# The front of an attention and feed-forward block on one core: program order, a first batch loaded alone, idle matmuls, an earlier norm, and first copies on three queues

## The chip, the cores and the metric

The kernel runs on one core of a Trainium2 chip. The core has a matrix engine (TensorE, PE in the profile; its weight loads are a row of their own, PEld), a vector engine (DVE), a scalar engine (ACT), a general engine (POOL) and a sync engine (SP), each with its own instruction queue that it works through in order. SP, ACT and POOL can also issue DMA transfers. An engine waits for another, or for a transfer, on a semaphore. The metric is the device time of one execution in microseconds (us), as the median of several runs. Smaller is better.

## What is computed

The reference is a block of attention and a gated feed-forward net over 4 batches of 1024 tokens of width 256, with 16 heads of 16. All of it is in 32-bit floats.

```python
def block(x):
    x = x + layernorm(attention(layernorm(x)))
    return x + layernorm(feed_forward(layernorm(x)))

def attention(x):                      # 16 heads of 16
    q, k, v = split(x @ Wqkv.T)
    scores = q @ k.T / sqrt(16)
    e = exp(clip(scores - max(scores), -50, 50))
    return (e / (sum(e) + 1e-6) @ v) @ Wout.T

def feed_forward(x):                   # w1, w2, h1, h2, w3 hold -1, 0 and 1
    h = silu(x @ w1.T * s1) * (x @ w2.T * s2)
    h = gelu(h @ h1.T * s3)
    h = gelu(h @ h2.T * s4)
    return h @ w3.T * s5
```

## The kernel before

`tile_fast` does the whole work; `tile_general` behind it runs only if checks on the data fail, which they do not here. A batch is cut into 2 halves (h) of 512 tokens, a half into 4 tiles of 128 tokens. The 16 heads are 4 groups (g) of 4.

**The front.** For batch 0, and for each half, a *prologue* makes: the norm's statistics (`gather`, L92 and L93: 4 tiles on DVE; `root`, L100 on DVE and L102, a power, on POOL); the normalised tokens `xn` (`apply`, L110, 4 instructions on DVE); their transposes (`pt`, L295, 8 on PE, copied into `xT` by ACT, L256); and, for the first 8 heads, the projections `p` to k and then q (L314, a pair of matmuls each, which the trace shows as 4 records). Each projection is split into a high part (ACT, L256: `ck0hi`, `cq0hi`) and a low part (DVE, L318: `ck0lo`, `cq0lo`). From these, small DMAs build the *stacks* `sk` and `sq` (L403): 16 partitions of 512 elements each, 16 DMAs for k and 16 for q in each half, dealt in turn to the queues of SP and POOL. `pv` (L305) makes the values of two token tiles at a time, 4 steps in all for a batch, and `slots` (L419, POOL) copies them into `vaug`, from which the weighing matmuls read.

**Order.** The set-up of the kernel, down to the rings, is put in order by a scheduler. The part under `with tc.manual_schedule()` stands as written: both halves' norms first, then for each half `apply`, transposes, projections and copies, then two `pv` steps (half of `v`), the first `slots` copy, the stacks of group 1 (`stack(0, 1)`, 32 DMAs on SP) and the output weights (`load_wo`, 16 DMAs on SP).

**The loads.** SP loads `x` of batch 0 (4 DMAs: for each half one of 128 KB and one of 384 KB), then four scales and `w3s`, then `x` of the batches 1 to 3 (12 DMAs). ACT issues one load of the q and k weights, `slotted` (1024 KB), from which POOL copies the used columns into `wqk_sb` (L188), and then `wv`. The pool that holds `slotted` is closed after this, and the pool `work`, in which `xn` and `xT` lie, opens at the same place of memory: the first `xn` waits for the copies out of `slotted`.

**Attention.** The loop goes over 512 score tiles, three at a time. For each, two matmuls make the scores (`s`, L441), ACT takes the exponential (`e`, L442) and four pairs of matmul records add the weighed values (`acc`, L449). The score tiles share three PSUM buffers (`ps`, tag "big"). One call of `side.take()` after each three tiles lets chains of *side steps* advance: at most one step that uses PE in each call, and after as many calls as the step's `gap`. The side steps hold the rest of batch 0's prologue (values, the projections of heads 8 to 15, then *flags*: checks of the size of the scores, `pn` at L350 with its maximum `norm` on DVE at L351, and `pr` at L366), the prologue of the next batch (`later["chain"]`), and checks of the feed-forward weights. Batch 0's side steps, `pn` and `pr` too, take their PSUM from the same three buffers as the scores. At the end of a unit of 16 tiles, `po` (L468, L470) divides by the sums.

**The feed-forward net** runs after all attention, from about half of the span on; none of its lines is touched.

Of the kernel before, what the change touches and what calls it, by code (L numbers as in the profile page):

```python
# [9 lines left out]
F32 = mybir.dt.float32  # L10
# [8 lines left out]
P = 128  # L19
HEADS = 16  # L20
DH = 16
SLOT = 32
# [8 lines left out]
SAFE = 25.0  # L31
FULL = 32.0
EARLY = 256
SPREAD = 32.0
NQ = 512
WIDE = 1024
# [77 lines left out]
def tile_fast(ctx: ExitStack, tc: tile.TileContext, x, wqk, wv, wo, w1, w1s, w2, w2s, h1, h1s, h2, h2s, w3, w3s, out, bad):  # L114
# [22 lines left out]
        t, n = NH + (TPQ - 1) * h, TPQ * h  # L137
        return (slice(n, n + 1), view[:, h : h + 1, :]), (slice(n + 1, n + TPQ), view[:, t : t + TPQ - 1, :])

    def load_x(b):  # L140
        view = x[b].rearrange("(t p) d -> p t d", p=P)
        for h in range(NH):
            for at, tokens in pieces(h, view):
                nc.sync.dma_start(out=xs[b][:, at, :], in_=tokens)

    load_x(0)
    ident = const.tile([P, P], F32, name="ident")
    make_identity(nc, ident)
    ones = const.tile([P, 1], F32, name="ones")
# [10 lines left out]
    misses = const.tile([P, counts + B * 2], F32, name="misses")  # L160
    nc.vector.memset(misses, 0.0)
    rounded = {n: dram.tile(list(w.shape), F32R, name=f"{n}_r") for n, w in weights.items()}
    scales = {}
    for name, w in (("w1", w1s), ("w2", w2s), ("h1", h1s), ("h2", h2s)):
        scales[name] = const.tile([P, HC], F32, name=f"{name}_scale")
        nc.sync.dma_start(out=scales[name], in_=w)
    w3s_sb = const.tile([P, D], F32, name="w3s_sb")
    nc.sync.dma_start(out=w3s_sb, in_=w3s.partition_broadcast(P))


    keep = ctx.enter_context(tc.tile_pool(name="keep", bufs=1))
# [6 lines left out]
    with ExitStack() as actx, ExitStack() as rctx:  # L178
# [4 lines left out]
        wo_sb = aw.tile([P, DC, D], F32, name="wo_sb")  # L183
        with tc.tile_pool(name="load", bufs=1, side="right") as load:
            slotted = load.tile([P, DC, 2, HEADS, SLOT], F32, name="slotted")
            nc.scalar.dma_start(out=slotted, in_=wqk.rearrange("(c p) (k h s) -> p c k h s", p=P, k=2, s=SLOT))
            for c in range(DC):
                nc.gpsimd.tensor_copy(wqk_sb[:, c], slotted[:, c, :, :, 0:DH])  # L188
        nc.scalar.dma_start(out=wv_sb, in_=wv.rearrange("(c p) d -> p c d", p=P))

        def load_wo(c):
            for h in range(HPT):
                r = SLOT * (HPT * c + h)
                nc.sync.dma_start(out=wo_sb[DH * h : DH * (h + 1), c, :], in_=wo[r : r + DH, :])

        for b in range(1, B):
            load_x(b)


        cq = {(w, m, k): keep.tile([P, S], F32R, name=f"c{'qk'[w]}{m}{k}") for w in range(2) for m in range(DC) for k in ("hi", "lo")}  # L200
# [9 lines left out]

        rp = rctx.enter_context(tc.tile_pool(name="ring", bufs=1))
        ring = [rp.tile([P, 2, 2, NQ], F32, name=f"e{i}") for i in range(RING // 2)]

        on = [aw.tile([P, TPQ, D], F32, name=f"on{h}") for h in range(NH)]

# [11 lines left out]
        def check_weights(n, c):  # L227

            k = blocks.index((n, c))
            st = {}  # L230

            def rows(w):
                return w[c * P : (c + rows_at_once[n]) * P, :].rearrange("(i p) d -> p i d", p=P)

            def load():
                st["w"] = work.tile([P, WIDE], F32, tag="w", name="w", bufs=1)
                nc.gpsimd.dma_start(out=st["w"].rearrange("p (i d) -> p i d", i=rows_at_once[n]), in_=rows(weights[n]))

            def cast():
                st["r"] = work.tile([P, WIDE], F32R, tag="wr", name="wr", bufs=1)  # L240
                nc.gpsimd.tensor_copy(st["r"], st["w"])

            def count(j):
                def run():
                    w, r = (t[:, NQ * j : NQ * (j + 1)] for t in (st["w"], st["r"]))
                    i = k * (WIDE // NQ) + j
                    nc.vector.scalar_tensor_tensor(w, w, 1.0, r.bitcast(F32), ALU.mult, ALU.not_equal, accum_out=misses[:, i : i + 1])
                    if NQ * (j + 1) == WIDE:
                        nc.gpsimd.dma_start(out=rows(rounded[n]).bitcast(F32), in_=st["r"].bitcast(F32).rearrange("p (i d) -> p i d", i=rows_at_once[n]))

                return run

            return [Step(load, 0, False), Step(cast, 3, False)] + [Step(count(j), 1, False) for j in range(WIDE // NQ)]
# [140 lines left out]
        def copies(g, w, c0=0, c1=S):  # L394

            m, i = g // GPT, g % 2

            def copy(u, j, n):
                def run(queue):
                    k = "hi" if (j // 2 == 0 if w == 0 else j % 2 == 0) else "lo"  # L400
                    r = (g % GPT) * HPG * DH + (2 * u + n) * DH
                    o = n * ROWS + j * DH
                    queue.dma_start(out=stacks[w, i, u][o : o + DH, c0:c1].bitcast(F32), in_=cq[w, m, k][r : r + DH, c0:c1].bitcast(F32))  # L403

                return run

            return [copy(u, j, n) for u in range(2) for j in range(PARTS) for n in range(2)]

        def stack(b, g):
            for w in (1, 0):  # L410
                for copy in copies(g, w):
                    copy(nc.sync)
            stacked[g % 2] = b, g

        def slots(b, g, t0=0, t1=NT):


            def run():
                nc.gpsimd.tensor_copy(  # L419
                    vaug[g % 2][:, t0:t1, :, 0:DH], cv[:, t0:t1, HPG * DH * g : HPG * DH * (g + 1)].rearrange("p t (h e) -> p t h e", e=DH)  # L420
                )
                slotted[g % 2] = b, g, t1

            return run
# [148 lines left out]
        def begin(b):  # L573

            if b + 1 < B:
                norm, xt, qk, v, flags = prologue(b + 1, misc, to_vector)

                qk1 = sum(qk[1], [])
                qk1[0].gap = 3
                later["rest"] = v, qk1 + [Step(lambda: side.add(flags), 0, False)]  # L580
                later["chain"] = side.add(sum((norm[h] + xt[h] for h in range(NH)), []) + sum(qk[0], []))

        def unit_end(b, g, h):

# [40 lines left out]
        def halves(pool, name):  # L625
            return [pool.tile([P, HC, NQ], F32R, name=f"{name}_{k}") for k in ("hi", "lo")]
# [178 lines left out]
                chain = side.add(finish(n, ffn["a"]), True)  # L805
            side.flush()

        with tc.manual_schedule():
            norm, xt, qk, v, flags = prologue(0, lambda n: ps.tile([P, 2, NQ], F32, tag="big", name=n)[:, 0, :], to_scalar)
            queues = [nc.sync, nc.gpsimd]  # L810
            for h in range(NH):
                for step in norm[h]:
                    step.run()
            for h in range(NH):
                for step in xt[h]:
                    step.run()
                for w, step in zip((1, 0), qk[0][h]):
                    step.run()
                    for i, copy in enumerate(copies(0, w, h * NQ, (h + 1) * NQ)):
                        copy(queues[i % len(queues)])  # L820
            stacked[0] = 0, 0
            for step in v[: len(v) // 2]:
                step.run()
            slots(0, 0, 0, NT // 2)()
            stack(0, 1)
            for c in range(DC):
                load_wo(c)
            side.add(v[len(v) // 2 :] + [Step(slots(0, 0), 0, False), Step(slots(0, 1), 0, False)] + sum(qk[1], []) + [Step(lambda: side.add(flags), 0, False)])
            begin(0)
            side.add([s for k in blocks for s in check_weights(*k)])  # L830
            made = seen = weighed = 0

            def make(end):

                nonlocal made
                for k in range(made, min(end, len(tiles))):
                    assert k - weighed < RING
                    exponentials(k)
                    made = k + 1

            while weighed < len(tiles):
                n = made
                make(n + TURN - side.borrowed)
                if made == len(tiles):
                    n = made
                for k in range(seen, n - 1, 2):
                    rise(k)
                    seen += 2
                while weighed + 2 <= n:
                    b, g, h, c, _ = tiles[weighed]  # L850
                    if c == 0:
                        accs[b, g, h] = ps_acc.tile([P, NQ], F32, tag="acc", name="acc")
                    weigh(weighed, accs[b, g, h])
                    weighed += 2
                    if c == NT - 1:
                        unit_end(b, g, h)
                        if n < len(tiles):
                            break
                make(n + TURN)
                if weighed < len(tiles):  # L860
                    side.take()

            load_weights("h1", range(HC // 2, HC))
            rctx.close()
            ffn["a"] = halves(ctx.enter_context(tc.tile_pool(name="fa", bufs=1, reuse_waits="tile")), "ha")
            feed_forward()


@with_exitstack
# [233 lines left out]
```

## Time and profile before

The median of 3 runs is 1353.05 us (1352.49 to 1354.52). The profiled execution took 1352.66 us, of which its span on the core is 1350.9 us.

| | busy us | share of the span |
|---|---|---|
| PE | 1273.3 | 94% |
| PEld | 799.0 | 59% |
| DVE | 732.5 | 54% |
| ACT | 684.1 | 51% |
| POOL | 159.7 | 12% |

| in the front | us from the span's start |
|---|---|
| first statistics of `x` | 3.45 |
| first `xn` | 11.86 |
| first transpose | 12.33 |
| first projection | 14.53 |
| first copy into a stack (SP) | 18.97 |
| first score matmul | 31.16 |
| first weighing matmul (`acc`) | 35.94 |

A line of the timeline has the start, the length, the engine, the line of the code, the operation, output and inputs, the shapes, and the number of merged instructions; in brackets stands the idle time before them and what ended it. A "q" after an engine's name (SPq) marks its queue issuing DMAs. In a table of windows each pair is the busy time of one engine and, in brackets, its instructions; PEclk is the share of the full clock that TensorE was granted. Ends of matmuls are modelled, so records that follow each other closely can overlap on paper.

### The profile page before, as it was taken

Reading aid. Unit: us, or ns where it says so; the run is one execution under the profiler, and the core shown is the slowest. Engines: PE = TensorE matmul, PEld = TensorE weight load, DVE = VectorE, ACT = ScalarE, POOL = GpSimd, SP = SyncE. Lnnn points to the kernel's source line nnn. Section 1 sums busy time; section 2 is a strip of 40 time slices with the busy share of each in tenths; the row PEclk is TensorE's granted clock in tenths of the full one; section 3 lists DMA queues with packets and bytes.
Section 4 is the critical chain, followed back from the end, with each engine's and each line's share of the span. In section 5 each row is a group of like instructions: output and inputs, shape, how many; then the busy total and the mean of one; then the engine's idle time right before and its main releaser. Section 6 shows DMA issues by size and latency. Waiting matters only on the chain.

```text
span 1350.9 us, 18751 instructions
## 1 busy us (share of the span) xinstructions
PE 1273.3 (94%) x7034; PEld 799.0 (59%) x7034; DVE 732.5 (54%) x1553; ACT 684.1 (51%) x820; POOL 159.7 (12%) x200
## 2 busy tenths in 40 slices
PE   5989999899899999989999999999999999999995
PEld 3333434343343433333478888888888888888884
DVE  3466568755697565735573452725436364363533
ACT  2677787676777678888842231413224141231410
POOL 6241133210421012000000000000000000000000
PEclk9989999899999999999999999999999999999998
DMA  7554344542445432336130000000000000000000
GB/s 215 130 113 110 80 111 91 141 103 60 129 108 133 94 51 48 50 65 195 54 134 1 1 16 0 17 1 0 16 1 16 0 14 3 0 16 0 17 0 19
DMA packets 38390, 79.62 MB, mean 59 GB/s; under 512 B 11280, under 2 KB 21136, under 8 KB 38288
## 3 DMA queue, kind: packets, MB, share of 16 engines
q1 hardware_dynamic: 30384, 52.88, 18.1%
q0 software_dynamic: 7360, 24.12, 5.3%
q10 hardware_dynamic: 544, 1.31, 0.3%
q8 instruction: 58, 0.95, 0.3%
q14 instruction: 44, 0.36, 0.1%
HBM read 28.98 MB, written 15.73 MB: 33 GB/s over the span
## 4 chain that ended last, share of the span: by engine, by line
PE 76%; DVE 12%; ACT 7%; issue 2%; POOL 1%; DMA 1%; SPq 1%; ACTq 0%; POOLq 0%; DVEq 0%
PE ph L686 35%; PE acc L449 13%; PE s L441 8%; ACT e L442 5%; PE p L314 5%; PE pz L739 4%; PE pg L686 3%; PE py L506 2%; PE pv L305 2%; DVE top L458 2%; DVE sg L702 2%; PE po L470 1%; DVE st L92 1%; DVE ha_lo L691 1%; DVE o L259 1%
## 5 line engine op out<-in xcount | busy, mean ns | idle before, releaser
L442 ACT ACTIVATE e<-s 128x1024 f32<-128x1024 f32 x512 | 484.9, 1032 | 143.4 <-PE s L441 128.0
L449 PE MATMUL acc<-e,vaug 128*32 128x512 f32 x2048 | 258.0, 607 | 0.1
L722 ACT ACTIVATE a<-ph,h_scale 128x512 f32<-128x512 f32 x128 | 81.0, 685 | 307.3 <-PE ph L686 307.3
L441 PE MATMUL s<-sq,sk 64*128 64x512 f32 x1024 | 195.9, 452 | 28.0 <-ACT e L442 20.3
L686 PE MATMUL ph<-hb_lo,h 128*128 128x512 f32 x512 | 199.7, 390 | 0.0
L686 PE MATMUL ph<-hb_hi,h 128*128 128x512 f32 x512 | 199.6, 390 | 0.0
L441 PEld LDWEIGHTS s<-sq,sk 64*128 64x128 f32 x1024 | 87.5, 185 | 164.5 <-ACT e L442 121.0
L458 DVE TENSOR_TENSOR top<-top,e 128x512 f32<-128x512 f32 x192 | 146.4, 762 | 29.7 <-ACT e L442 23.4
L102 POOL TENSOR_TENSOR rstd<-ve,minus_half 128x4 f32<-128x4 f32 (+1 forms) x33 | 37.1, 1125 | 772.5 <-DVE ve L100 772.5
L723 DVE CAST ha_hi<-a 128x512 fp32r<-128x512 f32 x64 | 27.1, 424 | 158.2 <-ACT a L722 158.2
L449 PEld LDWEIGHTS acc<-e,vaug 128*32 128x32 f32 x2048 | 49.7, 109 | 106.1 <-issue 96.7
L686 PEld LDWEIGHTS ph<-hb_hi,h 128*128 128x128 f32 x512 | 96.2, 188 | 20.1
L686 PEld LDWEIGHTS ph<-hb_lo,h 128*128 128x128 f32 x512 | 96.2, 188 | 20.0
L686 PE MATMUL ph<-ha_hi,sq 128*128 128x512 f32 x256 | 102.0, 399 | 0.4
L686 PE MATMUL ph<-ha_lo,sq 128*128 128x512 f32 x256 | 100.0, 391 | 0.0
L686 PE MATMUL ph<-ha_lo,sk 128*128 128x512 f32 x256 | 99.9, 390 | 0.0
L686 PE MATMUL ph<-ha_hi,sk 128*128 128x512 f32 x256 | 99.9, 390 | 0.0
L702 DVE SCALAR_TENSOR_TENSOR sg<-pg,w_scale,sg 128x512 f32<-128x512 f32 x64 | 47.1, 746 | 47.9 <-ACT sg L700 47.8
L700 ACT ACTIVATE sg<-pg,w_scale 128x512 f32<-128x512 f32 x64 | 43.3, 688 | 56.7 <-DVE ha_lo L691 47.4
L723 DVE CAST hb_hi<-a 128x512 fp32r<-128x512 f32 x64 | 27.0, 422 | 82.2 <-ACT a L722 82.2
L314 PE MATMUL p<-xT,wqk_sb 128*128 128x512 f32 x128 | 65.1, 635 | 0.2 <-ACT xT L256 0.2
L686 PEld LDWEIGHTS ph<-ha_hi,sq 128*128 128x128 f32 x256 | 48.2, 188 | 12.7 <-DVE sg L702 3.3
(144 smaller groups left out, 1679.6 us busy)
## 6 DMA issues: line engine op xcount, KB each, us to landing
w<-in_h_dram POOLq DMA_DIRECT2D x16, 512.0 KB, 4.4
h_r<-wr POOLq DMA_DIRECT2D x16, 512.0 KB, 3.6
sk<-ck1hi SPq DMA_DIRECT2D x64, 64.0 KB, 2.3
sk<-ck1lo SPq DMA_DIRECT2D x64, 64.0 KB, 2.3
sq<-cq1hi SPq DMA_DIRECT2D x64, 64.0 KB, 2.3
sq<-cq1lo SPq DMA_DIRECT2D x64, 64.0 KB, 2.3
h<-h_r SPq DMA_DIRECT2D x8, 512.0 KB, 7.1
sk<-ck0hi SPq DMA_DIRECT2D x56, 64.0 KB, 2.3
```

The costliest lines, as they stand in the source:

```text
L102: nc.gpsimd.tensor_tensor(rstd[:, :n], ve[:, :n], self.minus_half[:, :n], ALU.pow)
L314: nc.tensor.matmul(pp, wqk_sb[:, c, w, HPT * m : HPT * (m + 1), :], st["xT"][:, c, h * NQ : (h + 1) * NQ], start=c == 0, stop=c == DC - 1)
L441: nc.tensor.matmul(s[:, a, :], stacks[1, g % 2, u][r, c * P : (c + 1) * P], stacks[0, g % 2, u][r, h * NQ : (h + 1) * NQ], start=True, sto ...
L442: nc.scalar.activation(pair(k)[:, u], s, AF.Exp)
L449: nc.tensor.matmul(acc[SLOT * i : SLOT * (i + 1), :], vaug[g % 2][:, c, i, :], pair(k)[:, i // 2, i % 2, :], start=c == 0, stop=c == NT - 1)
L458: nc.vector.tensor_max(top, top if c > 1 else pair(k - 2)[:, :, :, 0:P], pair(k)[:, :, :, 0:P])
L686: nc.tensor.matmul(p, homes[n][c][:, m * P : (m + 1) * P], half[:, c, :], start=c == 0 and k == 0, stop=c == len(homes[n]) - 1 and k == 1)
L700: nc.scalar.activation(sg, p[:, 0, :], AF.Silu, scale=scales["w1"][:, m : m + 1])
L702: nc.vector.scalar_tensor_tensor(sg, p[:, 1, :], scales["w2"][:, m : m + 1], sg, ALU.mult, ALU.mult)
L722: nc.scalar.activation(a, p[:, j, :], AF.Gelu, scale=scales[n][:, m : m + 1])
L723: nc.vector.tensor_copy(o[0][:, m, :], a)
L739: nc.tensor.matmul(p[t], half[:, c, t * P : (t + 1) * P], homes["w3"][c], start=c == 0 and k == 0, stop=c == HC - 1 and k == 1)
```

## The change

All of `tile_fast` after the pools now stands in the order in which it is written (`manual_schedule` opens before the first load). The parts:

1. **Loads.** Only batch 0 is loaded ahead, all on SP: half 0 of `x`, the k half of `slotted` (512 KB), half 1 of `x`, the q half of `slotted`. ACT copies each half into `wqk_sb`. Batch 1's `x` is loaded behind the first copies, and `load_wo`, the batches 2 and 3, the scales and `w3s` behind `stack(0, 1)`.
2. **Idle matmuls.** A memset fills 128x512 of the ring's first buffer with zeros, and four matmuls on it stand first on PE, into the PSUM buffer of the side steps; nothing reads their result.
3. **Early norm.** Half 0's norm and its `xn` now stand ahead of half 1's norm on DVE; half 1's `xn` stands between half 0's k and q copies.
4. **Three queues.** The 16 copies of a k or q half are dealt in groups of eight as ACT, POOL, SP, POOL, SP, POOL, SP, POOL.
5. **Values.** One `pv` step instead of two stands ahead of the first scores; the second, and the first `slots` copy, become the first side steps. The chain of batch 1 starts four calls later.

```diff
-    load_x(0)
+    ctx.enter_context(tc.manual_schedule())
+    load_x(0, [0])
...
-            nc.scalar.dma_start(out=slotted, in_=wqk.rearrange("(c p) (k h s) -> p c k h s", p=P, k=2, s=SLOT))
-            for c in range(DC):
-                nc.gpsimd.tensor_copy(wqk_sb[:, c], slotted[:, c, :, :, 0:DH])
+            for w in (1, 0):
+                nc.sync.dma_start(out=slotted[:, :, w], in_=wqk.rearrange("(c p) (k h s) -> p c k h s", p=P, k=2, s=SLOT)[:, :, w])
+                nc.scalar.copy(wqk_sb[:, :, w], slotted[:, :, w, :, 0:DH])
+                if w:
+                    load_x(0, [1])
...
-        for b in range(1, B):
-            load_x(b)
+        def load_rest():
+
+            for c in range(DC):
+                load_wo(c)
+            for b in range(2, B):
+                load_x(b)
+            for name, w in (("w1", w1s), ("w2", w2s), ("h1", h1s), ("h2", h2s)):
+                nc.sync.dma_start(out=scales[name], in_=w)
+            nc.sync.dma_start(out=w3s_sb, in_=w3s.partition_broadcast(P))
...
+        zeros = ring[0][:, 0, 0]
+        nc.vector.memset(zeros, 0.0)
...
-                later["chain"] = side.add(sum((norm[h] + xt[h] for h in range(NH)), []) + sum(qk[0], []))
+
+                later["chain"] = side.add([Step(lambda: None, 0 if b else 4, False)] + sum((norm[h] + xt[h] for h in range(NH)), []) + sum(qk[0], []))
...
-            queues = [nc.sync, nc.gpsimd]
-            for h in range(NH):
-                for step in norm[h]:
-                    step.run()
-            for h in range(NH):
-                for step in xt[h]:
-                    step.run()
-                for w, step in zip((1, 0), qk[0][h]):
-                    step.run()
-                    for i, copy in enumerate(copies(0, w, h * NQ, (h + 1) * NQ)):
-                        copy(queues[i % len(queues)])
-            stacked[0] = 0, 0
-            for step in v[: len(v) // 2]:
+        queues = [nc.scalar] + [nc.gpsimd, nc.sync] * 3 + [nc.gpsimd]
+
+        idle = misc("idle")
+        for _ in range(WARM):
+            nc.tensor.matmul(idle, zeros[:, 0:P], zeros, start=True, stop=True)
+        normalise = [steps[: TPQ // 2] for steps in xt]
+        for step in norm[0] + normalise[0] + norm[1]:
+            step.run()
+        for h in range(NH):
+            for step in xt[h][TPQ // 2 :]:
                 step.run()
-            slots(0, 0, 0, NT // 2)()
-            stack(0, 1)
-            for c in range(DC):
-                load_wo(c)
-            side.add(v[len(v) // 2 :] + [Step(slots(0, 0), 0, False), Step(slots(0, 1), 0, False)] + sum(qk[1], []) + [Step(lambda: side.add(flags), 0, False)])
+            for w, step in zip((1, 0), qk[0][h]):
+                step.run()
+                for i, copy in enumerate(copies(0, w, h * NQ, (h + 1) * NQ)):
+                    copy(queues[i % len(queues)])
+                if w and h + 1 < NH:
+                    for step in normalise[h + 1]:
+                        step.run()
+        stacked[0] = 0, 0
+        v[0].run()
+        load_x(1)
+        stack(0, 1)
+        load_rest()
+        early = [v[1], Step(slots(0, 0, 0, NT // 2), 0, False)]
+        side.add(early + v[2:] + [Step(slots(0, 0), 0, False), Step(slots(0, 1), 0, False)] + sum(qk[1], []) + [Step(lambda: side.add(flags), 0, False)])
```

The loop over the tiles is moved out by one level of indentation and is otherwise as it was.

## The prediction

> **What bounds the kernel now.** I read the page's slices and chain first, then the timeline of the first 45 us, where the change is, then the stretch of batch 0's checks, and last the granted clock in 3.41 us windows.
>
> ```profile
> PE   5989999899899999989999999999999999999995
> PEclk9989999899999999999999999999999999999998
> PE 76%; DVE 12%; ACT 7%; issue 2%; POOL 1%; DMA 1%; SPq 1%; ACTq 0%; POOLq 0%; DVEq 0%
> ```
>
> PE is full from the second slice on (a slice is 33.8 us), and holds 76% of the chain. So work that leaves the front and goes into the attention isn't saved; only PE's idle and slow time can be. The first slice has half of its time idle.
>
> ```profile
> 0.74 1.97 SPq L144 DMA_DIRECT2D x<-in_x_dram  x4
> 2.75 0.49 SPq L166 DMA_DIRECT2D w_scale<-in_w1s_dram  x1
> 6.21 1.16 POOL L188 COPY wqk_sb<-slotted 128x512 f32<-128x512 f32 x2 [4.05 <-DMA slotted<-in_wqk_dram]
> 7.31 0.43 DVE L92 BATCH_NORM_STATS2 st<-x 128x6 f32<-128x256 f32 x1 [3.22 <-DMA x<-in_x_dram]
> 11.86 1.38 DVE L110 TENSOR_SCALAR xn<-x,mv,rstd 128x256 f32<-128x256 f32 x4
> 14.53 5.82 PE L314 MATMUL p<-xT,wqk_sb 128*128 128x512 f32 x8
> 19.24 0.72 POOL L403 DMA_DIRECT2D sk<-ck0hi  x1 [6.49 <-ACT ck0hi L256]
> 24.07 3.70 PE L314 MATMUL p<-xT,wqk_sb 128*128 128x512 f32 x8 [0.25 <-ACT xT L256]
> 31.16 1.26 PE L441 MATMUL s<-sq,sk 64*128 64x512 f32 x6
> 34.97 0.41 POOL L419 COPY vaug<-cv 128x256 f32<-128x256 f32 x1
> 35.94 1.07 PE L449 MATMUL acc<-e,vaug 128*32 128x512 f32 x8
> ```
>
> The chain to see: loads until 7.31, both halves' statistics until 11.55, `xn` at 11.86. The same eight projection records take 5.82 us cold and 3.70 us warm. POOL issues 32 copies from 19.24 to 34.97 without a gap (0.48 us each), copies `vaug` until 35.38, and only then can `acc` start.
>
> ```profile
> 77.28 0.73 PE L441 MATMUL s<-sq,sk 64*128 64x512 f32 x4
> 80.67 0.80 PE L441 MATMUL s<-sq,sk 64*128 64x512 f32 x2 [2.67 <-DVE norm L351]
> 81.40 1.93 PE L449 MATMUL acc<-e,vaug 128*32 128x512 f32 x8
> ```
>
> ```profile
> 18.83:22.24 3.41, 1.67 (x5) 0.52 (x3) 1.92 (x4) 0.71 (x2) 2.99 (x6) 1.00 0.50 125
> 76.85:80.27 3.42, 1.16 (x12) 0.30 (x4) 3.21 (x10) 2.38 (x3) 0.77 (x1) 1.00 0.60 101
> 80.27:83.68 3.41, 3.00 (x12) 0.91 (x13) 1.23 (x3) 1.02 (x1) 3.39 (x5) 0.50 0.76 112
> 83.68:87.09 3.41, 3.41 (x16) 1.72 (x18) 2.10 (x7) 1.06 (x2) 2.99 (x4) 0.50 0.95 322
> 247.52:250.93 3.41, 1.54 (x12) 0.34 (x10) 3.17 (x13) 3.16 (x4) 0.42 (x1) 1.00 0.64 105
> ```
>
> Second column PE busy, third from the end the clock. A window with PE busy 1.16 or 1.54 us is followed by half clock, one with 1.67 is not; the clock returned after a window that was full, not after one with 3.00. A pause is thus paid twice.
>
> **The change, part by part.** "A" is the start of the first `xn`, 11.86 before.
>
> *Loads and early norm.* Half 0's statistics no longer hold A back: half 0's x, 0.52 MB at the head of the queue, is moved by 3.7 (DMA column: 0.45 MB by 3.5, 0.65 by 4.0); with 0.6 for the landing, three more tiles of statistics and `ve` (7.31 to 9.22, so 1.9) and a power on POOL (1.03), `xn` could start near 7.5. But `xn` lies where `slotted` lay, and waits for ACT's copy of the q half, the last of the six loads. These are the same 2.10 MB as before, which the DMA column completes at 8.0; the first scale, behind x on SP's queue, had landed at 9.15 (issued 2.75, 6.4 to landing). So q lands between 8.0 and 9.15; ACT's copy of 512 elements costs 0.60 (the `xT` row) and 0.1 to start. A is 8.7 to 9.9, and I take 9.7, since the tail counts for the last load: **-2.2**. The far bound is one queue alone at its slowest microsecond, 248 GB/s (13 to 14 us): 2.0 + 8.5, tail 1.1, copy 0.7: A = 12.3, or +0.4. POOL's 1.16 us of copies had cover and goes free.
>
> *Idle matmuls.* The memset lies before any x has landed: nothing. Four matmuls are 8 records of 0.85 us cold (spacing within L314's 5.82), 6.8 us from about 1.4. The clock opens with the end of the first full window, 3.4 to 6.8 us after the start, and halves the rest; they end at 6.5 to 8.2, before A, and delay nothing. If they end later than A + 0.5, the excess is paid in full. What they bring: first transpose at A + 0.47 = 10.2, so PE pauses 2 to 3.7 us. By the windows above (1.54 us busy of 3.41 is too little) the clock mostly closes again, and the projections run cold as before. I take **0**; the other end is warm projections: k's high part was done 7.1 after `xn` cold (18.94) and 5.1 warm (26.69 against 21.62), so -2.0. The Trainium skill, "TensorE: Matmul & The Clock Gate", section "What's actually happening", has the clock close only after an idle window of about 3.4 us and lets a shorter pause pass. The row speaks against it: a pause of 2.67 us closed it. By the rule the projections would mostly stay warm and the sum be lower by those 2.0.
>
> *Three queues.* Of the 32 copies of a half SP now issues 12 instead of 16, ACT 4 and POOL 16 as before. ACT's come in twos behind `ck0hi` and `cq0hi`, at about 0.5 us each (its earlier issues took 0.46 and 0.37), while ACT is idle for 1.12 to 2.44 us behind each of the four anyhow, waiting for PE: nothing; without this cover 1 us per pair. So POOL's chain, 7.4 us after A to the first issue, 15.7 for 32 copies, 0.41 for `vaug`, is unchanged: A + 23.5. The scores come earlier (PE's chain: A + 15.7 with one `pv` less; the last copies at A + 17), but `acc` must wait for POOL. Before it came at A + 24.1, 0.56 after `vaug`; now PE is ready first: **-0.5** (0 to -0.5).
>
> *One `pv` moved.* The front had no room to gain from it (above), so it counts where it lands. By the built order every step shifts by one slot, the row of steps regains the old order at score tile 90 (of 512), and a slot that held no PE step is used up. A slot with a step takes 3.9 to 4.1 us, one without is held by three `e` (2.85) plus waits, 2.9: **+1.2**; from 1.0 to 2.4 (1.93 of PE and a 0.41 wait for the buffer).
>
> *Loads moved behind copies.* On SP, 24 copies, 4 of x1, 32 of group 1 at 0.62: from A + 7.8 to about 55, landed by 57. Group 1 is first read at score tile 32, about 71 now: 14 us spare. Then 29 issues (wo, x2, x3, scales, w3s), 18 us, to 73, when group 2's copies become due; these need not land before tile 64, at about 107, and take 20. Batch 1's statistics stand behind `cq1lo` on DVE, at about 48; x1 lands by 41. All **0**; without cover each us late costs one.
>
> *The check `pn`.* Before, it cost a pause of 2.67 and then half clock: s, acc, po, po, s, acc after it took 0.80, 1.93, 1.12, 1.09, 1.22, 2.27 instead of 0.51, 1.07, 0.66, 0.66, 0.73, 1.92: 2.9 more, 5.6 in all. In the built order it moves from before tile 33 to before tile 39, after a `po`. From `po`'s start T on DVE (62.55 as the model): multiply done T + 3.3 (65.83), two statistics 1.1, `ve` 0.2, power 1.04 to 1.41, two `xn` 0.73, `norm` 0.69: T + 7.2 to 7.5. PE reaches tile 41, which needs that buffer, at T + 5.9. Pause 1.3 to 1.6, and half clock less often, say 3 in 10: 1.6 + 0.9 = 2.5. **-3.1** (0 to -5.6: the old cost, or none). `pr` moves to tile 87; its wait was 0.35 and stays.
>
> The sum: -2.2 - 0.5 + 1.2 - 3.1 = **-4.6**, so 1352.66 - 4.6 = 1348.1 for an execution like the profiled one, which lies 0.4 under the median: **1348.5**.
>
> **The rivals.**
> 1. *The front stays warm.* For it: 18.83:22.24, half idle, kept its clock. Against: the pause is longer. -6.6: 1346.5.
> 2. *The pause at `pn` stays in full.* DVE has `xn` before `norm`, and POOL the power. For it: the same engines made it before; against: the ops counted. -1.5: 1351.5, no change to be told (0.2%, or 2.7 us, is what a measurement of this kernel can tell).
> 3. *Slower: a second half-clock stretch.* `pn` keeps its 5.6, and the other moved check (second `pn`, or `pr`) gets a pause like 250's, 1.7, with 2.9 behind it: -1.5 + 4.6 = +3.1: 1356.2. It decides where a pause leaves PE under 1.6 us busy of a window. For it: the second `pn` already had 0.63 of wait. Against: no x statistics stand before it.
> 4. *No gain at A.* The loads on one queue at 248 GB/s (+0.4 instead of -2.2), the rest as in 2: +1.1: 1354.2.
>
> **How the numbers follow.** Forecast 0.50 (0.42 of it faster, its own range 1346 to 1351), rival 1 0.17 (all faster), rival 2 0.15 (0.04 faster, 0.11 same), rival 3 0.11 (0.09 slower, 0.02 same), rival 4 0.07 (0.06 same, 0.01 slower). The forecast's remaining 0.08 is same. Faster 0.63, same 0.27, slower 0.10. The range runs from rival 1 with `pn` free (1346.5 - 2.5, so 1344) to rival 4 at 1354; outside are rival 3 and the tails.
>
> **What would show it.** First `xn` at 9.7, ended by ACT's copy; idle records over by 8.2, then a pause on PE of over 2 us, and projections again at 0.85 each (warm: 0.43); POOL's 32 copies without gap and `acc` waiting for `vaug`, near 33.3; tile 32 some 2 us earlier than before; a pause of about 1.5 before tile 41 at full clock. From tile 90 on all should be shifted alike. Wrong would be: `xn` after 12, `acc` not ended by POOL, or another half-clock stretch.

## Result and profile after

The changed kernel takes 1349.90 us in the median of 7 executions (1348.01 to 1352.52) against 1353.05 (1350.74 to 1354.52): a ratio of 0.9979, 95% interval 0.9968 to 0.9991. Its profiled execution took 1349.57 us, with a span of 1347.8; before it was 1352.66 with a span of 1350.9.

The timeline of the front after the change (start, duration, engine, line, operation; in brackets the idle time of the engine before it and what ended it):

```profile
1.57 5.66 PE L825 MATMUL idle<-e 128*128 128x512 f32 x8 [1.57 <-DVE heads_bf L227]
...
8.88 0.62 ACT L187 COPY wqk_sb<-slotted 128x512 f32<-128x512 f32 x1 [2.19 <-DMA slotted<-in_wqk_dram]
9.59 1.38 DVE L111 TENSOR_SCALAR xn<-x,mv,rstd 128x256 f32<-128x256 f32 x4 [3.01 <-ACT wqk_sb L187]
10.06 1.73 PE L305 MATMUL pt<-ident,xn 128*128 128x128 f32 x8 [2.82 <-DVE xn L111]
12.11 5.40 PE L324 MATMUL p<-xT,wqk_sb 128*128 128x512 f32 x8 [0.31 <-ACT xT L266]
...
20.08 3.70 PE L324 MATMUL p<-xT,wqk_sb 128*128 128x512 f32 x8 [0.91 <-ACT xT L266]
...
25.44 0.51 PE L451 MATMUL s<-sq,sk 64*128 64x512 f32 x2
27.09 0.93 PE L451 MATMUL s<-sq,sk 64*128 64x512 f32 x4 [1.15 <-DMA sq<-cq0hi]
...
31.28 0.96 POOL L413 DMA_DIRECT2D sq<-cq0lo  x2
32.24 0.41 POOL L429 COPY vaug<-cv 128x256 f32<-128x256 f32 x1
32.70 1.84 PE L459 MATMUL acc<-e,vaug 128*32 128x512 f32 x8 [1.57 <-POOL vaug L429]
```

Up to here it went nearly as forecast. The first `xn` starts at 9.59 (11.86 before), released by ACT's copy of the last weights; in the other ten runs with these loads, described below, it starts between 9.66 and 10.41. The idle records end at 7.23, PE then stands for 2.82 us, and the projections take 5.40 us, cold as before (5.82). POOL issues to 32.24, and the first `acc` waits for `vaug`. The first score is 5.7 us earlier (25.44, 31.16 before), the first `acc` 3.2 (32.70, 35.94).

After that the lead runs away. The table has the start of some `e` tiles (ACT's exponentials, 512 in order) against the same tile of before's profile, in us, from the two traces (negative is earlier; e1, e12 and g1 are runs described below); the last column is the stretch from tile 20 to 92, in which the moved step sits, and behind which both kernels have the same order on PE.

| tile | 0 | 20 | 28 | 60 | 92 | 511 | 20 to 92 |
|---|---|---|---|---|---|---|---|
| changed kernel | -5.43 | -2.14 | +0.79 | -1.31 | -0.16 | -0.39 | +1.98 |
| e1 (one POOL instruction more) | -5.32 | -3.63 | -0.69 | -2.99 | -1.82 | -1.36 | +1.81 |
| e12 (moved step undone) | -4.16 | -3.37 | -3.23 | -5.25 | -5.06 | -4.70 | -1.69 |
| g1 (best) | -3.19 | -3.27 | -2.46 | -6.37 | -5.23 | -14.26 | -1.96 |

So of the span's 3.1 us, the attention holds 0.4. Where it went shows in the timeline from the unit's end near 80 us:

```profile
76.80 2.27 DVE L468 TENSOR_TENSOR top<-top,e 128x512 f32<-128x512 f32 x2
79.00 0.41 DVE L93 BATCH_NORM_STATS2 st<-x 128x6 f32<-128x256 f32 x1
...
80.07 1.45 DVE L257 SCALAR_TENSOR_TENSOR w<-w,wr 128x512 f32<-128x512 f32 x1
...
81.45 1.51 DVE L468 TENSOR_TENSOR top<-top,e 128x512 f32<-128x512 f32 x1
82.89 0.68 DVE L269 TENSOR_SCALAR o<-acc 128x512 f32<-128x512 f32 x1
...
77.49 1.04 POOL L338 TENSOR_TENSOR sq<-cq0hi 128x512 bf16<-128x512 f32 x1
78.50 1.48 POOL L338 TENSOR_TENSOR sq<-cq1hi 128x512 bf16<-128x512 f32 x1
79.94 1.03 POOL L338 TENSOR_TENSOR sq<-ck0hi 128x512 bf16<-128x512 f32 x1
80.93 1.48 POOL L338 TENSOR_TENSOR sq<-ck1hi 128x512 bf16<-128x512 f32 x1
...
78.74 1.07 PE L459 MATMUL acc<-e,vaug 128*32 128x512 f32 x8
83.11 0.63 PE L478 MATMUL po<-ident,top 128*128 128x128 f32 x4 [3.31 <-DVE top L468]
```

PE ends `acc` at 79.81 and waits 3.31 us for DVE's `top`: a pause that the kernel before did not have here. DVE is late, and part of that is that two `top` took 2.27, `w` 1.45 and `top` 1.51 (0.69 each elsewhere) while POOL squared; the statistics beside them took their usual 0.41. The Trainium skill, "GPSIMD Engine Reference", section "1. Specifications", leads one to expect this: POOL shares its SBUF interfaces with VectorE, and there is contention with VectorE's instructions that have two SBUF inputs or run in a 2-port mode (`top` and `w` have two inputs, the statistics one).

The windows of the changed kernel (PE busy second, the clock third from the end) show the price:

```profile
9.00:12.38 3.38, 2.01 (x9) 1.22 (x10) 2.71 (x9) 1.42 (x3) 0.00 (x0) 1.00 0.30 78
29.45:32.86 3.41, 1.82 (x13) 0.74 (x15) 0.00 (x0) 3.19 (x5) 3.41 (x8) 1.00 0.54 122
32.86:36.27 3.41, 3.41 (x12) 1.50 (x5) 0.00 (x0) 0.47 (x1) 0.29 (x1) 0.50 0.78 227
80.65:84.06 3.41, 0.95 (x8) 0.84 (x8) 2.92 (x4) 0.68 (x1) 3.41 (x5) 1.00 0.60 105
84.06:87.47 3.41, 3.41 (x18) 1.09 (x20) 2.87 (x11) 1.94 (x2) 0.07 (x1) 0.50 0.96 247
```

Each of the three pauses is followed by half clock (the first from 12.38 to 15.79); the second, behind the wait before `acc`, and the third, behind the wait for `top`, were not forecast.

And where the rest of the 3.1 us came from stands at the very end. SP's last four stores, and the span, in before and in the changed kernel:

```profile
core 0 of [0], span 1350.9 us
1334.98 5.59 SPq L751 DMA_DIRECT2D out_dram<-z  x4
```

```profile
core 0 of [0], span 1347.8 us
1334.20 5.60 SPq L762 DMA_DIRECT2D out_dram<-z  x4
```

The last store's issue ends at 1340.57 and 1339.80, 0.77 apart; but from there to the end of the span it is 10.3 us and 8.0 us. POOL's records between them, in us:

```
                  wait ends   final drain starts   drain   last store to end
before             1341.19         1343.62          6.41        10.3
changed kernel     1340.27         1340.35          6.27         8.0
```

POOL waits for the stores. The next instruction, a drain, starts 2.4 us later in before, with 8 KB fetches on an instruction queue in the gap, and at once in the changed kernel. Before's trace holds 274 POOL instructions, the changed kernel's 273.

### The profile page after: what moved, and what is told of

The parts are those of the page before. It is cut to its first block, busy times and chain, and to the rows that moved or that the text cites. A ratio compares the mean times of both kernels' runs of the same rounds, so it can differ in the third digit from the quotient of the medians.

```text
span 1347.8 us, 18771 instructions
## 1 busy us (share of the span) xinstructions
PE 1279.4 (95%) x7042; PEld 799.8 (59%) x7042; DVE 736.0 (55%) x1554; ACT 685.1 (51%) x822; POOL 159.2 (12%) x198
## 4 chain that ended last, share of the span: by engine, by line
PE 75%; DVE 12%; ACT 7%; issue 2%; POOL 2%; DMA 1%; SPq 1%; ACTq 0%; POOLq 0%; DVEq 0%
PE ph L697 35%; PE acc L459 13%; PE s L451 8%; ACT e L452 5%; PE pz L750 4%; PE p L324 4%; PE pg L697 3%; PE py L516 2%; PE pv L315 2%; DVE sg L713 2%; DVE top L468 2%; PE po L480 1%; DVE ha_lo L702 1%; DVE st L93 1%; DVE o L269 1%
```

## The experiments

**The end: one POOL instruction more, or fewer (e1, e2, f1).** e1 is the changed kernel with one more:

```diff
             vaug.append(t)
+        nc.gpsimd.memset(vaug[1][:, :, :, DH : DH + 1], 1.0)
```

> The changed kernel with one more POOL instruction (a second memset of the ones columns of the second vaug, early, under the loads), so that POOL has as many instructions as in the kernel before. Theory A (the end of the program depends on where POOL's last instructions lie): the time between the last store's issue and the end of the span is back at 10.3 us (8.0 in the changed kernel, 10.3 before), the rest as in the changed kernel, so the span is 1347.8 + 2.3 = 1350.1 and the time 0.8 us below before. Rival B (the end is chance, or belongs to the stores): the end stays within 0.5 us of 8.0 or varies between executions, the time is 3.1 us below before. Rival C (all of the gain is in the work): the last pz starts 3 us earlier than before.

e2 is the kernel before, with one fewer:

```diff
-            nc.gpsimd.memset(t, 0.0)
-            nc.gpsimd.memset(t[:, :, :, DH : DH + 1], 1.0)
+            on = nc.vector if i else nc.gpsimd
+            on.memset(t, 0.0)
+            on.memset(t[:, :, :, DH : DH + 1], 1.0)
```

> The kernel before with one POOL instruction fewer (both memsets of the second vaug are done by DVE, under the loads), as many as in the changed kernel; nothing of the change is in it. Theory A (place of POOL's last instructions): the time between the last store's issue and the end of the span falls from 10.3 to 8.0 us and the time is 2.3 us below before, so this alone gives most of the changed kernel's 3.1. Rival B (chance, or the stores): end at 10.3, time as before within 0.5 us. Score tile 0 starts at 31.7 and tile 511 as before under both.

Measured: e1 1351.89 us, ratio 1.0000 (0.9992 to 1.0009): the whole gain is gone. e2 1348.53, ratio 0.9973 (0.9961 to 0.9985): as much as the changed kernel, with nothing of the change in it (3.6 us below before, where 2.3 was expected; the interval, 2.0 to 5.3, holds that). The last stores of e1, then of e2:

```profile
core 0 of [0], span 1348.9 us
1333.18 5.60 SPq L763 DMA_DIRECT2D out_dram<-z  x4
```

```profile
core 0 of [0], span 1348.9 us
1335.28 5.59 SPq L752 DMA_DIRECT2D out_dram<-z  x4
```

1348.9 - 1338.78 = 10.1 in e1, 1348.9 - 1340.87 = 8.0 in e2. Is it a count, or a border? f1 repeats e1's memset eight times.

> The changed kernel with eight more POOL instructions (eight small memsets of the second vaug's ones, under the loads). With one more, the end took 10.2 us and the gain was gone. Theory A1 (a border in POOL's program: the wait for the stores and the drain behind it lie on the two sides of it, and the part behind it is fetched only when it is reached; with eight more, both lie behind it and are fetched together while POOL waits anyhow): the end is 8.0 us again and the time is some 3 us below before. Rival A2 (every instruction beyond a count makes the end longer): 10.2 us or more, time as before.

f1: 1347.76, ratio 0.9969 (0.9955 to 0.9984), from the last store to the end 7.8 us. In these runs:

```
POOL instructions   272        273              274          281
kernels             e6, g2     changed, e2      before, e1   f1
wait to drain       0.06       0.06             2.4, 2.5     0.06   us
last store to end   8.0        8.0              10.3, 10.2   7.8    us
```

The other runs have 271 to 273 instructions and end 7.9 to 8.3 us behind the last store. So it is a border in POOL's program that falls between the wait and the drain with 274 instructions only. A smaller gap in the records marks the same place: with 273 it stands one instruction later, behind the drain (0.36 us), with 272 two later (0.39), with 271 three later (0.38). That the drain is then fetched late is read from the fetches in the gap; which unit sets the border was not tried.

**The idle matmuls (e3).** `WARM = 0`.

> The changed kernel without the four idle matmuls. Theory A (they bring nothing, since PE pauses 2.8 us before the projections and runs these cold): the eight projection records of the first half take 5.4 to 5.8 us as with them, score tile 0 starts at 26.3 and the time is that of the changed kernel within 0.5 us. It would even be shorter in the front if a window lost less later: the clock opens 3.4 us or more after the first transposes, so the second half's projections may be cold for 1 us more. Rival D (the idle matmuls do part of the work): score tile 0 at 28.3, 2 us later, and since acc waits for POOL's 32 copies and vaug, acc starts as late as vaug, 32.7 to 34.

1348.56, ratio 0.9975 (0.9966 to 0.9984): as with them. Tile 0 starts at 27.0 (26.3 with them) and `acc` at 33.39 waits 1.58 us for POOL all the same. That is 0.7 us later, as is the first `xn` (10.27 against 9.59), which the idle matmuls don't touch; so they bring nothing. In this run PE did not run at half clock after `top`, and the check's pause came back behind it; its timeline:

```profile
82.18 0.63 PE L478 MATMUL po<-ident,top 128*128 128x128 f32 x4 [3.33 <-DVE top L468]
90.74 0.65 PE L451 MATMUL s<-sq,sk 64*128 64x512 f32 x2 [2.83 <-DVE norm L361]
```

So `pn` had kept its pause. In the changed kernel it looked smaller (0.63), for the most part because PE, at half clock, came to it 1.6 us later after the start of `po`.

**The wait for POOL (e6).** The first copy into `vaug` on DVE, which is idle there:

```diff
-        def slots(b, g, t0=0, t1=NT):
+        def slots(b, g, t0=0, t1=NT, on=nc.gpsimd):
...
-                nc.gpsimd.tensor_copy(
+                on.tensor_copy(
...
-        early = [v[1], Step(slots(0, 0, 0, NT // 2), 0, False)]
+        early = [v[1], Step(slots(0, 0, 0, NT // 2, nc.vector), 0, False)]
```

> The changed kernel with the first copy into vaug on DVE in place of POOL, where it stood behind 32 copies. Theory A (the first acc waits 1.57 us for POOL alone, and the half clock after it, 32.86 to 36.27, is the price of that wait, some 1.7 us): the wait is gone, no half clock around 33, score tile 8 starts 2.5 to 3.3 us earlier than in the changed kernel (36.6 against 39.6); what of that is left at the end of the attention is open, since the lead before it was lost there too. Rival E (the copies on SP end no earlier, or the stacks' landing holds the scores): tile 8 at most 0.5 us earlier. For the whole time A says -1 to -3 us against the changed kernel, E 0.

Tile 8 starts at 35.91 (39.68 in the changed kernel, 38.18 in e1), the wait is gone, and so is the half clock there. The lead of 6.0 at tile 20 fell to 1.0 at tile 92 by the same pauses at `top` (3.31) and `pn` (2.22), each with a half-clock window. Ratio 0.9971 (0.9960 to 0.9982), which can't be told from the changed kernel's 0.9979: hardly anything is left.

**The queues (e8).** `queues = [nc.sync, nc.gpsimd]`, as before.

> The changed kernel with the first copies on SP and POOL in turn, as before (16 each per half) in place of ACT, POOL and SP (4, 16 and 12). Theory A (POOL's 32 copies and vaug behind them hold the first acc, and SP is no limit): first acc within 0.3 us of the changed kernel's 32.7; the scores' own wait for the copies of the second half, 1.15 us, may grow by up to 1 us, hidden before acc. Rival H (ACT's queue was what let the first scores start): score tile 0 over 1 us later and acc too. Time: A the same within 0.5 us, H +1 us or more.

Theory A fell, and rival H held in the trace. Most of SP's issues took 0.59 to 0.62 us against POOL's 0.48, so with 32 of them SP is the later one: the scores wait for it, tile 0 starts at 27.74 instead of 26.32, tile 4 at 35.74 instead of 31.39, and `acc` at 35.45. Its timeline:

```profile
29.82 0.95 PE L451 MATMUL s<-sq,sk 64*128 64x512 f32 x4 [2.11 <-DMA sq<-cq0lo]
35.45 1.06 PE L459 MATMUL acc<-e,vaug 128*32 128x512 f32 x8
```

Some of it is filled by `pv`; at tile 20 the run is 1.1 us behind the changed kernel. Ratio 0.9997 (0.9986 to 1.0007), whose interval overlaps the changed kernel's. Taking eight issues off SP is what lets the scores start; that they must go to ACT was not tried.

**The moved `pv` (e5, e12).** e5 put both `pv` ahead of the scores but left the copy into `vaug` as a step.

> The changed kernel with both pv of the front ahead of the first scores, as in the kernel before (the moved step undone). Theory A (the moved pv takes a slot of the attention, which cost the lead 2.2 us at score tile 24, and in the front there is room for it, since the first acc waits for POOL): score tile 0 starts 1.0 to 1.9 us later than in the changed kernel, acc as late as before at 32.7 to 33, and from tile 24 on the lead over before is 2 us larger than in the changed kernel. What follows it (the pauses at the first top and pn) comes at other places and is open. Rival F (a slot more or less costs nothing, since the steps only fill idle time): same lead at tile 28 within 0.5 us. Time: A 1 to 2 us below the changed kernel, F the same.

It did not undo the move: the first slot now held no PE step, and the others kept their places. Tile 24 started 2.3 us later than in before, the time was 1352.22, ratio 0.9994 (0.9982 to 1.0007). e12 undoes it:

```diff
-                later["chain"] = side.add([Step(lambda: None, 0 if b else 4, False)] + ...
+                later["chain"] = side.add([Step(lambda: None, 0 if b else 3, False)] + ...
...
         v[0].run()
+        v[1].run()
         load_x(1)
+        slots(0, 0, 0, NT // 2)()
...
-        early = [v[1], Step(slots(0, 0, 0, NT // 2), 0, False)]
-        side.add(early + v[2:] + ...
+        side.add(v[2:] + ...
```

> The changed kernel with its moved step truly undone: both pv and the first copy into vaug ahead of the first scores, and the next batch's chain one slot earlier, so that PE's order is that of the kernel before from the second score slot on (the run with both pv in front had left the first slot empty instead and so undid nothing). Theory A (the moved step costs one slot of 1.1 to 2.2 us in the attention; the second pv in the front is hidden while acc waits for POOL; the pause at top comes from the new order): score tile 0 at 28 to 29 instead of 26.3, first acc at 33 as before, no loss at tile 24: the lead over before there is 2 to 3.6 as at tile 20; no pause of 3.3 at top but the old one of 2.7 at pn; at tile 511 the lead is 2 to 3.5 (1.4 or less in the changed kernel), less a half-clock window of 1.7 where one falls otherwise. Rival F (the lead is lost anyhow, to the same pauses): lead at tile 511 under 1.4. The end is 8.0 us as in the changed kernel. Time: A 1 to 2 us below the changed kernel, F the same.

1345.57, ratio 0.9953 (0.9935 to 0.9971). The second `pv` was free in the front (lead at tile 20: 3.37, e1 3.63), nothing is lost at tile 24, and the lead at 511 is 4.70. The old pause at `pn` was there (3.13 us), this time without half clock behind it, which had stood there in before from 80.27 to 87.09:

```profile
77.90 0.49 PE L451 MATMUL s<-sq,sk 64*128 64x512 f32 x2 [3.13 <-DVE norm L361]
```

So the gain is larger than theory A's 1 to 2 us, and part of it is the clock.

**The pause at `top` (f5, g2).** f5 moves POOL's squares two slots earlier and leaves PE's order alone:

```diff
-            flags = [Step(total(m), 1, False) for m in range(DC)]
+            sums, flags = [Step(total(m), 1, False) for m in range(DC)], []
             for h in range(NH):
-                flags += [Step(squares(w, m, h), 0, False) for w, m in kinds] + [Step(bound(h), 3)]
+                flags += [Step(squares(w, m, h), 0, False) for w, m in kinds] + ([] if h else sums) + [Step(bound(h), 3 if h else 2)]
```

> The changed kernel with the four squares on POOL two slots (about 8 us) earlier in batch 0's checks, ahead of the two sums on DVE; PE's order is the same. Theory A (the new pause of 3.3 us at the unit's end, po waiting for top, is DVE being late, and it is late because its top, w and top took 2.27, 1.45 and 1.51 while POOL worked on the squares, 2.5 us more than 1.36, 0.69 and 0.69): in the last 6 us ahead of that unit's end these take 0.69 each, the pause falls from 3.3 to under 1, and no half clock follows it. Rival G (DVE has simply too much to do there: sums, statistics, w): the pause stays over 2 us. Time: A -1 to -3 us against the changed kernel if no later pause takes it back, G the same.

```profile
78.42 1.47 DVE L468 TENSOR_TENSOR top<-top,e 128x512 f32<-128x512 f32 x2
...
81.47 1.21 DVE L349 TENSOR_REDUCE sum<-ck1hi 128x1 f32<-128x1024 f32 x1
82.60 0.68 DVE L468 TENSOR_TENSOR top<-top,e 128x512 f32<-128x512 f32 x1
...
83.43 0.63 PE L478 MATMUL po<-ident,top 128*128 128x128 f32 x4 [2.46 <-DVE top L468]
```

`top` is quick again (0.68; two take 1.47), and the pause is 2.46 instead of 3.31, 0.85 less. The edit also brings a `sum` of 1.21 just ahead of `top`, so this doesn't split the 3.31 cleanly into contention and amount of work. But without the contention most of the pause stayed, so rival G holds. Ratio 0.9968 (0.9956 to 0.9979), which can't be told from the changed kernel's. g2 therefore puts the sums behind the first `pn` (`+ [Step(bound(h), 3)] + ([] if h else sums)`), together with e6's edit and `WARM = 0`; the checks compute the same.

> The changed kernel without idle matmuls, with the first copy into vaug on DVE, and with the squares of each check ahead and the two sums behind the first pn, so that DVE has 2.4 us less to do ahead of the unit's end. Theory G (the pause of 3.3 at top was the amount of DVE's work in that stretch: with squares 8 us earlier it fell to 2.5 only, while a sum of 1.21 still lay just ahead of top): the pause at the second top (near 79) falls under 1 us and no half clock follows it. Theory A (it was the slowing by POOL, the other part of it): it stays near 2.5. With the wait for POOL gone too, G says a lead over before of 4 us or more at tile 36 to 48, and 2.5 to 4.5 left at tile 511; time 5 to 7 us below before with the end of 8.0. If the pause only moves on (to pn, as the one at pn moved to top), the lead at 511 is as in the run with DVE's copy alone.

The pause at the second `top` is gone: from 59 up to the wait at `pn`, which ends at 85.04, no wait is over 0.75 us. The edit moves squares and sums together, so it doesn't say what the sums alone would do. `pn` (2.08) and the next `top` (1.90), with half clock from 84.20 to 91.03 and from 101.27 to 104.68, still took the lead of 7.7 at tile 40 down to 0.4 at tile 92. At that `top` the contention is back: two took 2.96 while POOL did the squares of the next check. But the edit holds for every batch, and there it removed what nobody had looked at, a pause of 3.44 and one of 1.68 in before's second check:

```profile
239.24 0.66 PE L295 MATMUL pt<-ident,xn 128*128 128x128 f32 x4 [3.44 <-DVE xT L259]
...
251.16 1.08 PE L468 MATMUL po<-ident,top 128*128 128x128 f32 x4 [1.68 <-DVE top L458]
```

After each of them before ran a window at half clock, which g2 doesn't have (its clock stays open from 104.68 to 1330.06):

```profile
240.69:244.10 3.41, 3.41 (x18) 0.77 (x20) 2.23 (x4) 2.58 (x3) 0.81 (x1) 0.50 0.76 211
250.93:254.35 3.42, 3.19 (x16) 2.24 (x20) 1.83 (x6) 0.42 (x1) 2.11 (x3) 0.50 0.69 122
```

In g2 a pause of 1.59 is left at this check. 6.8 of the 8.8 us that g2 gains on before from tile 92 to tile 511 fall between tiles 150 and 192, at this place: 3.5 us less of pauses, and an estimated 1.7 us for each window that is no longer at half clock.

g2: 1339.89, ratio 0.9896 (0.9878 to 0.9913), twice the gain expected.

**The best version, and what the front is worth in it (g1, b1).** g1 is g2 with both `pv` and the copy in the front.

> As the run with DVE's copy and late sums, and with both pv and that copy ahead of the first scores, so that the attention holds one PE step fewer. If the moved step costs its slot (theory A), the lead over before at tile 28 is 1.1 to 2.2 us larger than there, though score tile 0 starts up to 1.9 later; without POOL in front of acc the later scores now cost, so the sum is -1 to +1 us against that run. pn lies a slot earlier, at tile 33, and may bring the old pause of 2.7 back: then 2 us slower than that run. Time: 4 to 7 us below before.

1336.82, ratio 0.9887 (0.9868 to 0.9905), the fastest of all. The pauses in its timeline, at `pn`, at this and the next unit's end, and in the second check:

```profile
76.57 0.49 PE L452 MATMUL s<-sq,sk 64*128 64x512 f32 x2 [1.00 <-DVE norm L362]
77.00 1.06 PE L460 MATMUL acc<-e,vaug 128*32 128x512 f32 x8
78.00 0.66 PE L479 MATMUL po<-ident,top 128*128 128x128 f32 x4
78.88 0.66 PE L481 MATMUL po<-ident,o 128*128 128x128 f32 x4 [0.23 <-DVE o L269]
...
96.89 0.63 PE L479 MATMUL po<-ident,top 128*128 128x128 f32 x4 [1.79 <-DVE top L469]
...
231.91 0.63 PE L305 MATMUL pt<-ident,xn 128*128 128x128 f32 x4 [1.59 <-DVE bounds L387]
```

1.00, 0.23, 1.79 and 1.59 us; the clock opened at 16.93 and stayed open to the end of the work. The median is 3.1 us below g2's, where -1 to +1 was expected, but the two intervals overlap; in the traces g1 leads g2 by 5.1 us at tile 511, and g2 ran three windows at half clock (84.20 to 91.03, 101.27 to 104.68) that g1 did not. b1 is the kernel before with the same edits and the same order on PE, so only the front differs; it too ran at full clock, from 25.99 to the end of the work.

> The kernel before with the same three edits as the best run so far (first copy into vaug on DVE, squares first and sums behind the first pn, the next batch's chain four slots later), so that PE's order of work is the same as there, and all that is left between the two is the front of the change itself: loads ahead, early norm, three queues, copies of the weights on ACT. POOL's program is short enough for the end of 8.0 us. Theory A (the front is worth its lead, 3.2 us at score tile 0 in that run, wherever no pause takes it back): score tile 0 at 31.7, a lead of 3.2 less over the whole attention, time 3 to 3.5 us above that run, so about 1340. Rival J (the front's lead is always taken back by later waits, as in the changed kernel): tile 511 and the time within 1 us of that run's 656.2 and 1336.8. Rival K (the waits of the checks behave otherwise from another start): tile 511 over 5 us later.

1340.76, ratio 0.9915 (0.9902 to 0.9929): 3.9 us above g1, where 3 to 3.5 was expected. Tile 0 starts at 31.92 and tile 511 at 659.39, against 28.57 and 656.18: 3.3 us at the start, 3.2 at the end. Theory A holds: the front's lead is real and lasts where no pause takes it back.

## Why the prediction was right and wrong

The forecast of 1348.5 stands 1.4 us from the 1349.9 measured, and the range holds it; but that is luck. More than two thirds of the gain is something else than was forecast, and of the signs that were to show the forecast wrong one came: another stretch of half clock.

- *A*: right. -2.2 forecast, -2.27 measured, ended by the copy that was named (-1.45 to -2.20 in the other runs with these loads). The far bound misread its row: 248 GB/s was not the slowest microsecond (10 to 11 us has 184), which didn't come to bear.
- *Idle matmuls*: right. The pause before the projections closed the clock again (2.01 us busy of 3.38), and e3 shows nothing lost without them.
- *`acc` held by POOL, -0.5*: right (32.70 against 33.3). That PE's wait of 1.57 us there could cost half clock too was missed. With half clock the lead at tile 20 was 2.14, without it (e1) 3.63; the terms up to there had summed to 2.7.
- *Three queues at nothing*: they were not without effect; with two the scores and `acc` would have waited for SP (e8).
- *One `pv` moved, +1.2*, and *the check `pn`, -3.1*: wrong, and these are the steps that failed. Together they were to give -1.9 between tiles 20 and 92; they gave +1.98 (+1.81 to +4.19 in e1, f1 and e3, which have the same order on PE there; -1.69 with the move undone, in e12). With the moved step the lead fell by 2.2 us from tile 20 to 24 and by 2.9 to 28 (0.3 and 0.1 without it, in e12), where 1.2 was taken; from tile 28 to 92 only 0.95 came back, where the `pn` term had 3.1. The `pn` term followed the one wait through the new order and had its pause shrink to 1.3 to 1.6 (its own parts add up to about 0.1 less). It did not ask what else DVE would be late with: the sums, the squares' contention and the statistics had moved onto the end of a unit, where `top` became the wait, for 3.31 and a half-clock window, and `pn` kept up to 2.83 behind it (e3). Rival 2 and rival 3 were both nearer: the pause stayed, and another came. The limit of 1.6 us busy in a window, by which rival 3 was to be decided, doesn't hold either: windows with 1.82 and 2.01 closed the clock.
- *The end*: not in the sum at all. The change moves two copies off POOL and leaves its program one instruction shorter; the prediction counted these copies as free, which they are where they stood, and did not ask what lies behind the last store. It is worth 2.2 to 2.3 us, 0.17%.

By itself, then, the changed work is worth nothing that could be measured (e1: 1.0000, 0.9992 to 1.0009), though its trace leads by 1.4 at tile 511. Part of this is the choice of execution: the one in e1's trace is the fastest of its 11 (1350.81 us, median 1351.89). The clock goes with the rest. Over the 177 executions of all kernels, within each kernel, the time falls by 0.79 us for each 0.001 of the mean granted clock (correlation -0.83). e1's mean clock was 0.9879, before's beside it 0.9897, which makes an estimated 1.4 us: the new pauses may cost as much clock as the front saved. That is a correlation; no run sets the clock alone.

## What to carry to other kernels

Before you credit a change with a gain, compare the two traces stage by stage, the stretch behind the last store included: here an instruction more or less gave all of the difference that could be measured. When a step moves, look at what the helping engine is late with next, not only at the wait that you meant to move. Work that no one waits for soon (here the sums, moved together with the squares) belongs behind the work that someone does.

## What the runs showed of the hardware

- One instruction more in POOL's program (274 against 273 in the trace) cost 2.2 to 2.5 us at the end, eight more nothing.
- The same wait may or may not cost clock. The changed kernel's 1.57 us before `acc` was followed by half clock; e1 with 1.69 kept it. Its timeline and windows:

```profile
32.85 1.07 PE L460 MATMUL acc<-e,vaug 128*32 128x512 f32 x8 [1.69 <-POOL vaug L430]
```

```profile
28.68:32.09 3.41, 2.46 (x13) 1.28 (x11) 0.00 (x0) 3.19 (x5) 3.41 (x8) 1.00 0.59 123
32.09:35.50 3.41, 2.65 (x16) 1.59 (x16) 0.00 (x0) 1.27 (x2) 1.20 (x3) 1.00 0.67 183
```

The windows lie elsewhere (the clock first opened at 5.56 in the changed kernel and at 4.78 in e1), so the pause was split between two, with 2.46 and 2.65 us busy, where the changed kernel had 1.82 in one. The Trainium skill, "TensorE: Matmul & The Clock Gate", section "What's actually happening", says that the window is free-running and does not start with the kernel; the runs agree. That it closes after an idle window is too narrow: windows with 1.82 and 2.01 us busy closed it here. The busy time in the records gives no limit either, since before's window with 1.67 kept its clock.
- DVE operations with two SBUF inputs took up to 2.2 times as long beside POOL's squares (1.51 against 0.69). `xn`, with one tensor input, was slowed too: in the changed kernel two took 2.17 us beside squares and 0.73 without.
